# Turning the rows of the output stage by DMA, as planes of half words, in a masked attention layer on one core

## The chip, the cores and the metric

The kernel runs on one core of one Trainium2 chip. The time is device microseconds of that core. The kernel before took 671.49 us (median of 3 runs, 670.96 to 672.75). All engines and queues below are those of the one core: TensorE (PE; its weight loads are PEld), VectorE (DVE), ScalarE (ACT), GpSimd (POOL) and SyncE (SP), which only issues DMAs here.

## What is computed

One layer of a graph attention network on 2708 nodes with 1024 features, all in float32. The reference, cut to what matters:

```python
h = maximum(layernorm(x), 0)
q, k, v = h @ W_q.T + b_q, h @ W_k.T + b_k, h @ W_v.T + b_v
z = (q @ k.T) / 32 * adj
z = where(z == 0, -10000, z)
out = x + relu(softmax(z, axis=1) @ v)
```

`adj` is a 2708 x 2708 matrix of zeros and ones with about four ones in a row, so a row of the softmax has few terms that count.

## The kernel before

**What is multiplied.** The kernel never forms k and v for all nodes. It forms M = W_q^T W_k once, then for each node q' = h M, takes the products of q' with the rows of h at the node's few neighbours, and sums these rows of h with the softmax's weights: u. Then out = x + relu(u W_v^T + b_v). A list of each node's neighbours is found by searching the rows of `adj`; nodes are sorted by their number of neighbours, so that a tile of 128 nodes needs few slots. There are 21 full tiles of 128 nodes (0 to 20), and a rest of 20.

**The units.** Both products with a 1024 x 1024 matrix are made two tiles at a time, as one Strassen step of 7 products of 128 x 512 by 512 x 512 blocks (function `multiply`). One pair of tiles is a *unit*. There are ten units of queries ("q") and then ten units of outputs ("o"), and one tile on its own at the end of each kind: tile 10 for the queries, tile 11 for the outputs (`alone`, from line 1199 on). The outputs go in the pairs (8,7), (6,5), (4,3), (2,0), (1,9), (15,14), (13,12), (16,17), (20,10), (18,19), and then 11. I call the ten output units o0 to o9. Each of the 7 products is four calls of matmul on one 128 x 512 bank (`add_block`, line 898); the profile counts two instructions for each of these float32 calls, so one product is 8 rows of it.

**What turns the rows.** TensorE needs the rows transposed: features on the partitions. In the kernel before, `half_turned` (line 338) makes four TensorE transposes of 128 x 128 into one PSUM bank. `blocks` calls it four times for a unit: `upper` turns the two halves of the first tile and copies them by ScalarE to the blocks a11 and a12 (`held`, line 641); `lower` turns the second tile, copies a22 by ScalarE and leaves a21 in PSUM. Then VectorE forms s1 = a22 + a21, s3 = a11 - a21, s2 = s1 - a11, s4 = a12 - s2 (line 645). The four sums and the blocks are the stationary operands of the 7 products. For the tile alone, `turned` does both halves with two ScalarE copies (line 345). The blocks of unit n+1 are made inside unit n: `upper` at step 0, `lower` at step 2, of the steps 0 to 6 between the products (`after`).

**Where u comes from.** `attention` is a stream of VectorE steps, cut up and put between the steps of the units by `advance`, with about 19 us of it in each output unit. For each tile: the scores (line 782, one instruction of 1024 elements for a slot), the exponential by ScalarE (line 798), the weights, a first scaled row by ScalarE (line 827; for two tiles line 821), and then the sum over the other slots on VectorE (line 835). GpSimd gathers the rows of h for this by indirect DMA (line 524) and loads q' (lines 526, 759). When the sum of a tile is done, and its unit is more than two units away, GpSimd's queue stores u to `u_dram` (line 844), and SP's queue loads it again as a row tile (line 1048), in step 4 of the unit two before the one that multiplies it. If the unit is nearer (`near`), u stays in SBUF (`held`) and is turned from there: of the 21 tiles, 15 go through DRAM and 6 are held (tiles 9, 14, 12, 16, 17, 10). Row tiles have 7 buffers (`ROWS`), blocks and sums have 14 (`small`).

**Order.** The order of VectorE's instructions is written by hand throughout. From the first late unit of queries on (`n == FIRST`), the other engines and queues get their order from the scheduler of the framework, which takes instructions by program order and by when it expects their inputs. Each engine and each queue runs its own instructions in order, and waits at the first whose input isn't there.

**What ScalarE does in a unit of the output stage, beside that.** It copies the bias into the two PSUM banks of the next unit (line 670), copies partial results between banks and SBUF (lines 911, 914, 927), and applies the relu on the way out (lines 988, 992, 996, 1004). GpSimd then adds x by an accumulating gather (line 981) and scatters the rows (line 736).

Of the kernel before, what the change touches and what calls it, by code (L numbers as in the profile page):

```python
# [10 lines left out]
FT = mybir.dt.float32  # L11
U32 = mybir.dt.uint32
I32 = mybir.dt.int32
U16 = mybir.dt.uint16
AF = mybir.ActivationFunctionType
ALU = mybir.AluOpType
AX = mybir.AxisListType

P = 128
NB = 512  # L20
# [37 lines left out]
def tile_preln_masked_attention(  # L58
# [12 lines left out]
    nc = tc.nc  # L71
    N, D = x.shape
    DC = D // P
# [4 lines left out]
    FULL = N // P  # L78
# [12 lines left out]
    dram = ctx.enter_context(tc.tile_pool(name="dram", bufs=1, space=bass.MemoryType.DRAM))  # L91
# [2 lines left out]
    h_dram = dram.tile([N, D], FT, name="h_dram")  # L94
    q_dram = dram.tile([EARLY * P, D], FT, name="q_dram")
    q_late = dram.tile([(FULL - EARLY) * P, D], FT, name="q_late")
    u_dram = dram.tile([FULL * P, D], FT, name="u_dram")
    m_dram = dram.tile([2, 2, P, 4, NB], FT, name="m_dram")
    tv_dram = dram.tile([4, P, 4, NB], FT, name="tv_dram")
    bp_dram = dram.tile([1, D], FT, name="bp_dram")  # L100
# [54 lines left out]
    t = 0  # L155
    while t < NT:
# [4 lines left out]
        t = e  # L161
# [14 lines left out]
    work = ph.enter_context(tc.tile_pool(name="work", bufs=3, side="right"))  # L176
# [9 lines left out]
    def row_tile(name):  # L186
        return work.tile([P, D], FT, tag="row", name=name, bufs=ROWS)
# [145 lines left out]
    def half_turned(xt, s):  # L333

        pt = psum.tile([P, 4, P], FT, tag="tp", name="pt")
        for c in range(4):
            k = s * 4 + c
            nc.tensor.transpose(pt[:, c, :], xt[:, k * P:(k + 1) * P], ident)  # L338
        return pt

    def turned(xt, name):

        hT = work.tile([P, D], FT, tag="hT", name=f"T_{name}", bufs=2).rearrange("p (c q) -> p c q", q=P)
        for s in range(DC // 4):
            nc.scalar.copy(hT[:, s * 4:(s + 1) * 4, :], half_turned(xt, s))
        return hT

    ordered = ExitStack()
    ordered.enter_context(tc.manual_schedule(engines={mybir.EngineType.Activation, mybir.EngineType.DVE}))
# [17 lines left out]
    with tc.tile_pool(name="w", bufs=1, side="left") as wp:  # L367
# [73 lines left out]
        if True:  # L441
# [7 lines left out]
            for o in range(DC):  # L449
# [6 lines left out]
                else:  # L456
                    k = o - H
# [58 lines left out]
    half = low.enter_context(tc.tile_pool(name="half", bufs=1, side="left", reuse_waits="tile"))  # L516

    def small(name):
        return half.tile([P, NB], FT, tag="half", name=name, bufs=14)
# [8 lines left out]
    rows_of = {}  # L528
    FIRST = EARLY // 2
# [11 lines left out]
    def put(lo, hi, puts):  # L541

        for t, (t0, n) in tiles_of(lo, hi):
            put = nc.gpsimd.indirect_dma_start(  # L544
                out=tab_dram[lo >= EARLY][:, :], out_offset=bass.IndirectOffsetOnAxis(ap=pos_i[:n, t:t + 1], axis=0),
                in_=tab[:n, t, :], in_offset=None)
            for other in puts:
                tc.declare_no_dep(put.ins, other.ins, reason="rows of a permutation")
            puts.append(put)
# [81 lines left out]

    behind = []

    def blocks(xa, xb, eng=None):


        ops = {}

        def held(name, bank):
            ops[name] = small(name).rearrange("p (c q) -> p c q", q=P)  # L640
            nc.scalar.copy(ops[name], bank)  # L641

        def put(name, a, b, op, eng=None):
            ops[name] = small(name).rearrange("p (c q) -> p c q", q=P)
            step = (eng or nc.vector).tensor_tensor(ops[name], a, b, op=op)  # L645
            if eng is None:
                behind.append(step)

        def upper():
            held("a11", half_turned(xa, 0))  # L650
            held("a12", half_turned(xa, 1))

        def lower():
            held("a22", half_turned(xb, 1))
            a21 = half_turned(xb, 0)
            put("s1", ops["a22"], a21, ALU.add)
            put("s3", ops["a11"], a21, ALU.subtract)
            put("s2", ops["s1"], ops["a11"], ALU.subtract, eng)
            put("s4", ops["a12"], ops["s2"], ALU.subtract, eng)

        return ops, upper, lower
# [15 lines left out]
    ops_of = {0: blocks(*rows_of.pop(0))}  # L677
# [153 lines left out]
    def sums(t):  # L831
        u, coef = us.pop(t)
        for s in range(0 if t in EMPTY else 1, K[t]):
            fill()
            chained(lambda: nc.vector.scalar_tensor_tensor(  # L835
                u, g_of[t][s], coef[:, at[t][s]:at[t][s] + 1], u, op0=ALU.mult, op1=ALU.add))
            free.append(g_of[t][s])
            yield 1.3
        fill()
        g_of.pop(t)  # L840
        if near(t):
            held[t] = u
        else:
            nc.gpsimd.dma_start(u_dram[t * P:(t + 1) * P, :], u)
        done.add(t)

    def attention(order):
# [35 lines left out]
    def near(t):  # L883

        return any(t in unit[1:] for unit in units[:now[0] + 3] if unit[0] == "o")
# [62 lines left out]
    lo, hi = slice(0, NB), slice(NB, D)  # L948
# [87 lines left out]
    def load_rows(unit):  # L1036
        kind, *pair = unit
        rows = []
        for t in pair:
            if t in held:  # L1040
                rows.append(held.pop(t))
                continue
            rows.append(row_tile(f"{kind}r_{t}"))
            if kind == "q":
                gather(rows[-1], h_dram[:, :], t, SLOTS, P)
            else:
                assert t in done, (t, done)
                nc.sync.dma_start(rows[-1], u_dram[t * P:(t + 1) * P, :])
        return rows

    products = []
# [42 lines left out]
    for n, unit in enumerate(units):  # L1094
        kind, ta, tb = unit
        now[0] = n
        if n == FIRST:
            ordered.close()
            ordered.enter_context(tc.manual_schedule(engines={mybir.EngineType.DVE}))
            nc.sync.dma_start(bp_dram, bp_sb[0:1, :])  # L1100
        share = (20.0 if kind == "q" else 19.0) / 7
        nxt = units[n + 1] if n + 1 < len(units) else None
        results = (q_results if kind == "q" else o_results)(ta, tb)

        def after(i):
            if (n, i) == (3, 2):
                pooled.close()
                counts()
            if (n, i) == (3, 3):
                with tc.issue_after(products[-1].ins):  # L1110
                    placed.append(sort())
            if (n, i) in ((4, 1), (4, 2)):
                ts_of_wv(2 * i - 2, 2 * i)
            if n == FIRST - 1 and i == 6:

                chain.append(behind[-1])
                next(stream)
            if (n, i) >= (FIRST, 1):
                advance(share)
            if nxt is not None:  # L1120

                if n == FIRST - 1 and i in (0, 2):
                    single_turned(i // 2)
                if i == (3 if n in (0, FIRST - 1) else 0):
                    ops_of[n + 1] = blocks(*rows_of[n + 1], nc.gpsimd if n + 1 < FIRST - 1 else None)
                    if n != FIRST - 1:
                        ops_of[n + 1][1]()
                if n != FIRST - 1 and i == (4 if n == 0 else 2):
                    ops_of[n + 1][2]()
                    rows_of.pop(n + 1)  # L1130
                    if n == last_q - 1:
                        all_rows()
                if i == 3:
                    if n == FIRST - 1:
                        single["banks"] = banks_for(bp_sb)
                    else:
                        banks_of[n + 1] = banks_for(bp_sb)
                if i == 4 and n + 2 < FIRST:
                    natural_rows(n + 2)
                if i == (2 if n == FIRST else 4) and n + 2 >= FIRST and n + 2 < len(units) and n + 2 not in rows_of:  # L1140
                    while units[n + 2][0] == "o" and not done.issuperset(units[n + 2][1:]):
                        advance(1.0)
                    rows_of[n + 2] = load_rows(units[n + 2])
            if (n, i) in steps_at:
                follow(steps_at[n, i])
            if (n, i) == (3, 4):
                searched()
            if n == last_q - 1 and i == 4:

                nc.sync.dma_start(bp_sb, bv.to_broadcast([P, D]))  # L1150
                nc.vector.tensor_sub(bp_sb[:, NB:], bp_sb[:, NB:], bp_sb[:, :NB])

            for k, at in enumerate(((0, 0), (0, 1), (0, 3), (0, 4), (0, 5), (0, 6), (1, 2))):
                if (n - last_q, i) == at:
                    place, src = ((M[:, 0, 0], of_wv(0, 0)), (T[:, 0], tv_dram[0]), (T[:, 1], tv_dram[1]),
                                  (M[:, 1, 0], of_wv(1, 0)), (M[:, 1, 1], of_wv(1, 1)), (T[:, 2], tv_dram[2]),
                                  (T[:, 3], tv_dram[3]))[k]
                    nc.sync.dma_start(place, src)

        multiply(n, results, after)  # L1160
# [39 lines left out]
    send(gather(y, x, alone, SLOTS, P))  # L1200
    tail(NT - 1)
    r, = load_rows(("o", alone))
    uT = turned(r, "alone")
    X, Z = banks_for(bp_sb)
    add_block(X, uT[:, 0:4, :], M[:, 0, 0])
    p1 = small("p1")
# [191 lines left out]
```

## Time and profile before

The profiled execution took 671.25 us in all, with a span of 669.5 us from the first to the last instruction; the 1.75 us around it are outside the trace. The granted TensorE clock was 0.997.

| What | Number |
|---|---|
| median of 3 runs (lowest, highest) | 671.49 us (670.96, 672.75) |
| the profiled execution, its span | 671.25 us, 669.5 us |
| VectorE busy | 518.4 us (77%) |
| ScalarE busy | 266.2 us (40%) |
| GpSimd busy | 403.1 us (60%) |
| moved by DMA | 194.29 MB, 290 GB/s |
| 120 + 48 transposes of rows u | lines "pt<-ident,or" and "pt<-ident,u" |

How to read it: a group of instructions is named by its line in the kernel, its engine, its operation, and what it writes and reads ("ps<-M,a" writes the bank ps, reads the matrix M and the block a). "xN" is the number of instructions. Matmuls overlap each other, so the mean of one (593 ns for 512 columns, 273 ns for a transpose) is longer than the distance between two of them (429 ns and 109 ns, from the chain: 8 of them in 3.43 and 0.87 us). The chain of work that ended last is followed from the last instruction back: at each step to what released it, or to the instruction before it on its engine.

### The profile page before, as it was taken

To read this page: it belongs to the slowest core of one execution; us is meant where nothing else is said; L and a number is where in the kernel's file an instruction comes from. 1 tells how busy PE (TensorE), PEld (TensorE's weight loads), DVE (VectorE), ACT (ScalarE), POOL (GpSimd) and SP (SyncE) were. 2 spreads that over 40 slices of the span, in tenths; PEclk is the share of its full clock that TensorE was granted. 3 is DMA by queue.
4 is the path that set the end of the run, shared out by engine and by line. 5 is a ranking of instruction groups with operands and counts; after the bars stand their busy time and mean duration, and the time that the engine had idled before them with its cause. 6 is when DMAs were issued, how large, how long until landed. Compare 5 with 4: busy or idle time off the path is not lost.

```text
span 669.5 us, 6372 instructions
## 1 busy us (share of the span) xinstructions
PE 653.4 (98%) x1764; PEld 332.4 (50%) x1764; DVE 518.4 (77%) x998; ACT 266.2 (40%) x399; POOL 403.1 (60%) x397
## 2 busy tenths in 40 slices
PE   7999999999999999999999999999999999999994
PEld 4777776444444444444444444444444444444441
DVE  5999879999589402799988899798788989989201
ACT  3467985855844212232242231432332433322220
POOL 2559991585513778676666366574674877872342
PEclk9999999999999999999999999999999999999998
DMA  8997989699566877799999999998997899794653
GB/s 344 407 360 262 368 302 374 235 372 352 204 218 227 279 242 229 270 373 348 326 340 352 403 411 386 293 306 247 333 294 191 235 304 356 212 284 141 175 136 117
DMA packets 62452, 194.29 MB, mean 290 GB/s; under 512 B 9721, under 2 KB 10073, under 8 KB 61514
## 3 DMA queue, kind: packets, MB, share of 16 engines
q0 software_dynamic: 34608, 109.77, 50.0%
q1 hardware_dynamic: 26794, 80.89, 32.5%
q10 hardware_dynamic: 1008, 3.15, 1.2%
q8 instruction: 16, 0.26, 0.2%
q14 instruction: 26, 0.21, 0.1%
HBM read 161.38 MB, written 45.46 MB: 309 GB/s over the span
## 4 chain that ended last, share of the span: by engine, by line
PE 83%; DVE 6%; issue 4%; DMA 3%; POOL 2%; ACT 1%; POOLq 0%; DVEq 0%
PE ps L898 37%; PE psy L898 26%; PE ps_y L397 6%; PE ps_x L397 5%; PE pt L338 4%; PE ps_z L397 4%; DVE junk L782 2%; DVE u L835 2%; DMA g<-h_dram,tab 2%; POOL g L524 1%; DMA out_dram<-y,tab 1%; DVE s L645 1%; DMA wlow<-in_wk_dram 1%; ACT a L641 0%; ACT u L827 0%
## 5 line engine op out<-in xcount | busy, mean ns | idle before, releaser
L524 POOL DMA_INDIRECT g<-h_dram,tab x106 | 129.9, 1226 | 46.7 <-issue 23.4
L898 PE MATMUL psy<-wlow,s 128*128 128x512 f32 x320 | 144.2, 593 | 1.3 <-ACT u L927 1.3
L898 PE MATMUL ps<-M,a 128*128 128x512 f32 x320 | 144.1, 593 | 0.1
L782 DVE SCALAR_TENSOR_TENSOR junk<-g,pq 128x1024 uint8<-128x1024 f32 x94 | 115.1, 1225 | 14.7 <-DMA pq<-q_dram,tab 12.6
L835 DVE SCALAR_TENSOR_TENSOR u<-g,coef,u 128x1024 f32<-128x1024 f32 x78 | 100.0, 1282 | 7.9 <-ACT u L827 4.9
L898 PEld LDWEIGHTS psy<-wlow,s 128*128 128x128 f32 x320 | 59.2, 190 | 69.4 <-issue 66.8
L898 PEld LDWEIGHTS ps<-M,a 128*128 128x128 f32 x320 | 59.3, 190 | 68.0 <-issue 67.2
L320 DVE FIND_INDEX8 at<-ones,adj 128x8 uint32<-128x685 f32 (+1 forms) x88 | 74.4, 865 | 0.0
L898 PE MATMUL psy<-wlow,a 128*128 128x512 f32 x160 | 72.3, 595 | 1.2 <-DVE q L963 0.8
L898 PE MATMUL ps<-wlow,s 128*128 128x512 f32 x160 | 72.1, 593 | 0.8 <-DVE s L645 0.7
L898 PE MATMUL ps<-M,s 128*128 128x512 f32 x160 | 71.9, 592 | 0.0
L981 POOL DMA_INDIRECT y<-in_x_dram,tab x21 | 37.0, 1763 | 49.2 <-ACT y L996 23.1
L309 ACT ACTIVATE sized<-adj 128x2708 uint8<-128x2708 f32 (+1 forms) x22 | 54.2, 2465 | 4.2 <-DMA adj<-in_adj_dram 4.1
L898 PEld LDWEIGHTS psy<-wlow,a 128*128 128x128 f32 x160 | 30.0, 190 | 40.3 <-issue 34.2
L898 PEld LDWEIGHTS ps<-wlow,s 128*128 128x128 f32 x160 | 30.2, 190 | 39.8 <-issue 37.1
L898 PEld LDWEIGHTS ps<-M,s 128*128 128x128 f32 x160 | 30.3, 190 | 37.6 <-issue 37.1
L257 POOL TENSOR_TENSOR hsum<-hsum,x 128x1024 f32<-128x1024 f32 (+1 forms) x17 | 40.3, 2371 | 0.4
L645 DVE TENSOR_TENSOR s<-a,pt 128x512 f32<-128x512 f32 x40 | 25.6, 682 | 17.5 <-ACT a L641 9.2
L641 ACT COPY a<-pt 128x512 f32<-128x512 f32 x60 | 33.2, 593 | 4.9 <-issue 3.3
L544 POOL DMA_INDIRECT tab_dram<-tab,pos_i x22 | 22.6, 1028 | 20.2 <-DVE pos_i L608 13.8
L827 ACT ACTIVATE u<-g,coef 128x1024 f32<-128x1024 f32 x16 | 18.4, 1148 | 34.8 <-DVE coef L826 26.8
L736 POOL DMA_INDIRECT out_dram<-y,tab x21 | 25.1, 1195 | 8.9 <-issue 5.8
(230 smaller groups left out, 871.6 us busy)
## 6 DMA issues: line engine op xcount, KB each, us to landing
adj<-in_adj_dram SPq DMA_DIRECT2D x21, 1354.0 KB
x<-in_x_dram SPq DMA_DIRECT2D x21, 512.0 KB
h_dram<-x POOLq DMA_DIRECT2D x21, 512.0 KB
u_dram<-u POOLq DMA_DIRECT2D x15, 512.0 KB
or<-u_dram SPq DMA_DIRECT2D x15, 512.0 KB
q_late<-q SPq DMA_DIRECT2D x10, 512.0 KB
pq<-q_late POOLq DMA_DIRECT2D x10, 512.0 KB
g<-in_wv_dram SPq DMA_DIRECT2D x16, 256.0 KB
```

The lines of the kernel that those rows point to most:

```text
L257: nc.gpsimd.tensor_add(hsum[:n], hsum[:n], xt[:n])
L309: nc.scalar.activation(sized[:n], a[:n, :, :PW], AF.Abs, accum_out=total[:n, t:t + 1])
L320: nc.vector.max_index(at[:n, t - first_t, g, :], ones[:n, 0:8], a[:n, g, :])
L338: nc.tensor.transpose(pt[:, c, :], xt[:, k * P:(k + 1) * P], ident)
L397: mm = nc.tensor.matmul(bank, a_tile(o + H * a[0], a[1], i), b(o), start=first and o == 0, stop=(o == H - 1), skip_group_check=True)
L524: return nc.gpsimd.indirect_dma_start(out=dst, out_offset=None, in_=src, in_offset=off, bounds_check=N - 1, oob_is_err=False)
L641: nc.scalar.copy(ops[name], bank)
L645: step = (eng or nc.vector).tensor_tensor(ops[name], a, b, op=op)
L782: chained(lambda: nc.vector.scalar_tensor_tensor(junk, g_of[t][s], 1.0, tq[t], op0=ALU.mult, op1=ALU.mult, accum_out=zall[:, t, s:s + 1]))
L835: chained(lambda: nc.vector.scalar_tensor_tensor(u, g_of[t][s], coef[:, at[t][s]:at[t][s] + 1], u, op0=ALU.mult, op1=ALU.add))
L898: mm = nc.tensor.matmul(bank, a[:, c, :], b[:, c, :], start=False, stop=(c == 3), skip_group_check=True)
L981: return nc.gpsimd.indirect_dma_start(out=y[:n], out_offset=None, in_=x, in_offset=off, compute_op=ALU.add)
```

## The change

The rows u are no longer turned by TensorE. When the sum u of a tile is done, ScalarE makes two copies of 128 x 1024 half words: the float32 words are looked at as pairs of 16-bit words, and all upper half words go to the left half of a second row tile (`split`), all lower half words to its right half. `split` is held or stored where u was; `u_dram` becomes a tensor of 16-bit words with rows of 2048. `load_rows` now issues a transposing DMA on SP's queue for every tile of an output unit, from DRAM or, for a held tile, from `split` in SBUF, into a new row tile: 16 blocks of 128 x 128 half words, the first 8 with the upper half words of the turned tile, the other 8 with the lower. `words_joined` puts the two planes together again: two ScalarE copies for each block of 128 x 512 words, each writing every second half word. `blocks_turned` takes the place of `blocks` for output units: eight such copies make a11, a12, a22 and a21, where three ScalarE copies from PSUM made a11, a12 and a22; a21 gets a buffer of `small` of its own. VectorE's four sums stay, with a21 read from SBUF and not from PSUM. For the tile alone, two copies of 128 x 1024 half words take the place of two copies from PSUM. The units of queries are turned by TensorE as before.

```diff
-    u_dram = dram.tile([FULL * P, D], FT, name="u_dram")
+    u_dram = dram.tile([FULL * P, 2 * D], U16, name="u_dram")
...
+    def words_joined(dst, turned, lo, hi):
+
+        words = dst.bitcast(U16).rearrange("p (k w) -> p k w", w=2)
+        for w in (1, 0):
+            nc.scalar.copy(words[:, :, w], turned[:, (1 - w) * D + lo:(1 - w) * D + hi])
+
+    def blocks_turned(ta, tb):
...
+        def joined_half(name, turned, s):
+            half = small(name)
+            words_joined(half, turned, s * NB, (s + 1) * NB)
+            ops[name] = half.rearrange("p (c q) -> p c q", q=P)
...
+        def upper():
+            joined_half("a11", ta, 0)
+            joined_half("a12", ta, 1)
+
+        def lower():
+            joined_half("a22", tb, 1)
+            joined_half("a21", tb, 0)
+            put("s1", "a22", "a21", ALU.add)
+            put("s3", "a11", "a21", ALU.subtract)
+            put("s2", "s1", "a11", ALU.subtract)
+            put("s4", "a12", "s2", ALU.subtract)
...
+        split = row_tile(f"split_{t}").bitcast(U16)
+        words = u.bitcast(U16).rearrange("p (k w) -> p k w", w=2)
+        for w in (1, 0):
+            nc.scalar.copy(split[:, (1 - w) * D:(2 - w) * D], words[:, :, w])
         if near(t):
-            held[t] = u
+            held[t] = split
         else:
-            nc.gpsimd.dma_start(u_dram[t * P:(t + 1) * P, :], u)
+            nc.gpsimd.dma_start(u_dram[t * P:(t + 1) * P, :], split)
...
         for t in pair:
-            if t in held:
-                rows.append(held.pop(t))
-                continue
             rows.append(row_tile(f"{kind}r_{t}"))
...
-                nc.sync.dma_start(rows[-1], u_dram[t * P:(t + 1) * P, :])
+                rows[-1] = rows[-1].bitcast(U16)
+                nc.sync.dma_start_transpose(rows[-1].rearrange("p (c r) -> p c r", r=P),
+                                            held.pop(t) if t in held else u_dram[t * P:(t + 1) * P, :])
...
-                    ops_of[n + 1] = blocks(*rows_of[n + 1], nc.gpsimd if n + 1 < FIRST - 1 else None)
+                    ops_of[n + 1] = blocks_turned(*rows_of[n + 1]) if nxt[0] == "o" else \
+                        blocks(*rows_of[n + 1], nc.gpsimd if n + 1 < FIRST - 1 else None)
...
-    uT = turned(r, "alone")
+    uT = work.tile([P, D], FT, tag="hT", name="T_alone", bufs=2)
+    words_joined(uT, r, 0, D)
+    uT = uT.rearrange("p (c q) -> p c q", q=P)
```

More of the change, by code (lines that the diff above doesn't have):

```diff
@@ L339, in half_turned @@
         return pt
[L341 to L346, printed above, removed]
     ordered = ExitStack()
@@ L632, in tile_preln_masked_attention, with put @@
     behind = []
+    def words_joined(dst, turned, lo, hi):
[3 more added lines that the diff above has]
+    def blocks_turned(ta, tb):
+        ops = {}
+        def joined_half(name, turned, s):
+            half = small(name)
+            words_joined(half, turned, s * NB, (s + 1) * NB)
+            ops[name] = half.rearrange("p (c q) -> p c q", q=P)
+        def put(name, a, b, op):
+            ops[name] = small(name).rearrange("p (c q) -> p c q", q=P)
+            nc.vector.tensor_tensor(ops[name], ops[a], ops[b], op=op)
+        def upper():
[8 more added lines that the diff above has]
+            put("s4", "a12", "s2", ALU.subtract)
+        return ops, upper, lower
     def blocks(xa, xb, eng=None):
```

## The prediction

> **What bounds the kernel now.** I read the page's shares first, then the chain that ended last, VectorE's waits, ScalarE's groups, and last the DMA queues. The page:
>
> ```profile
> PE 653.4 (98%) x1764; PEld 332.4 (50%) x1764; DVE 518.4 (77%) x998; ACT 266.2 (40%) x399; POOL 403.1 (60%) x397
> ...
> PE 83%; DVE 6%; issue 4%; DMA 3%; POOL 2%; ACT 1%; POOLq 0%; DVEq 0%
> ```
>
> TensorE is busy for 98% and makes 83% of the chain. The chain from 511 us on, in order of time (start, length, what):
>
> ```profile
> 511.36 0.69 DVE u L995
> ...
> 572.87 0.61 DVE p L991
> 573.53 3.70 PE psy L898 x8
> 577.23 0.88 PE pt L338 x8
> 578.10 3.43 PE psy L898 x8
> 581.54 0.88 PE pt L338 x8
> 582.41 6.87 PE ps L898 x16
> ...
> 642.65 0.93 PE pt L338 x8
> ```
>
> Two things are to be seen. From 573 on it is products and transposes without a gap: 8 transposes are 0.88 us of the path, twice in a unit. From 511 to 573 the chain runs through VectorE, and yet TensorE was idle for only 0.34 us at its end (573.53): in these 2.4 units both engines need the same time. VectorE's waits from 366 us (where the first rows u are turned) to 521, then from 521 to 625 (us in total, times, longest):
>
> ```profile
> DVE u L995 <- PE ps L898: 5.9, 4, 1.6
> DVE s L645 <- ACT a L641: 4.0, 3, 2.1
> DVE u L835 <- ACT u L827: 3.7, 3, 1.3
> DVE s L645 <- PE pt L338: 1.9, 1, 1.9
> DVE q L966 <- PE ps L898: 1.6, 1, 1.6
> DVE p L991 <- PE psy L898: 0.7, 3, 0.2
> ```
>
> ```profile
> DVE u L835 <- ACT u L827: 3.6, 3, 1.2
> DVE u L835 <- ACT u L821: 1.2, 1, 1.2
> ```
>
> Before 521 VectorE waits 5.9 + 1.9 + 1.6 + 0.7 = 10.1 us for TensorE, and 4.0 us for copies of turned blocks, which themselves follow TensorE. After 521 it waits for TensorE no more. So VectorE has 14.1 us in hand, and TensorE has most to give. No line has VectorE waiting for a gather.
>
> **What goes.** Each output unit has 16 transposes, 2 x 0.875 = 1.75 us of TensorE; ten units, 17.5 us, and 0.93 us for the tile alone: **18.4 us**, were TensorE the only bound. What is late next is VectorE. From the timeline, the step that frees TensorE for the last product of o8 (line 991) ended at 619.8, and TensorE started that product at 625.37. TensorE's new start, ahead by the nine units' and the query unit's transposes, is 625.37 - 17.5 = 607.9. VectorE without the 14.1 us of waits would be there at 605.7. But it can't use all of them: laying its work by units beside the new 24.03 us of a unit (56 x 0.429), it is still early by 1.1, 1.8 and 0.8 us in o2 to o4, so 3.7 us stay as waits, and it gets there at 609.4. The gain at that point is 625.37 - 609.4 = 16.0 us, and with the 0.9 us of the tile alone **16.9 us**.
>
> **What is added to ScalarE.** ScalarE's groups from 366 to 625 us give the prices:
>
> ```profile
> L641 ACT COPY a<-pt 128x512 f32<-128x512 f32 x30 | 16.6, 592 | 0.0
> L670 ACT COPY ps<-bp_sb 128x512 f32<-128x512 f32 x20 | 12.0, 602 | 0.3
> L827 ACT ACTIVATE u<-g,coef 128x1024 f32<-128x1024 f32 x10 | 11.5, 1147 | 9.0 <-DVE coef L826 5.5 <-DVE m L825 2.5 <-DMA g<-h_dram,tab 1.1
> ```
>
> The first group is what goes, 30 copies. No row copies half words, or with a step of two. Nearest are 0.60 us for 512 elements (line 670) and 1.05 for 1024 (line 221, 1050 ns, SBUF to SBUF). I take these, one element at a time whatever its size. Half of it would follow if bytes counted, twice if a step of two cost two; neither shows in a row. In this window ScalarE was busy 84 of 259 us. Added: 14 of the 21 tiles' splits (the first seven sums end before 366), 28 x 1.05 = 29.4; 80 halves joined, 80 x 0.59 = 47.2; gone, 30 x 0.59 = 17.7. That makes 143 us of some 243, 59% where it was 32%. ScalarE alone would bind only if each half-word copy cost 2.3 times the row.
>
> Its bulk lies beside other work; its order does not. A split waits for the last sum of VectorE with all behind it in ScalarE's queue, and two splits are 2.1 us. Behind them stand the evictions that TensorE needs (lines 911, 914, 927, with 6.9 to 10 us until the bank is used again, two or three products of 3.43) and the first scaled row (line 827), for which VectorE stands idle. In 366 to 625 VectorE waits for that row 7 times, 8.5 us in all, each time just its length. With ScalarE busy for 59%, I add one split's length to each: 7 x 1.0 = **7 us**; none is the lower end, both splits before each of the 14 first rows of the window, 14 x 2.1 = 29 us, the upper. The joins are hidden: rows u arrive a unit ahead (loaded from 344 us, turned at 370; from 386, turned at 422), they no longer wait for TensorE, and the 4.0 us of waits for line 641 are in the sum above already. If they are joined just before VectorE's s1 all the same, 2.4 us for a22 and a21 in place of one copy costs 1.8 us in each unit, 18 us.
>
> **What moves in the queues.** GpSimd's store waits for two splits more (2.1 us), and behind it in that queue stand gathers; they run some instructions ahead of VectorE, which waited for none, so zero, with a gather's issue (1.2 us) in each of 21 tiles, 25 us, as the upper end. Row tiles: 6 are asked for in a unit, where 4 were, out of 7; a tile lives for about 0.7 of a unit, so they go round. Six more loads of 512 KB go through SP's queue, which waits idle for the stores anyway.
>
> **The transposing load** is the unknown. A plain load of 512 KB, in a quiet stretch (the DMA queues from 628 to 636):
>
> ```profile
> q1 hardware_dynamic: 144, 0.52, 17.6%
> ```
>
> It was issued at 628.36 and moved from 629.2 to 631.0: 1.8 us. That is the lower end. For the upper end the nearest row of small pieces is the reload of the sorted table (line 554): 10 tiles x 128 = 1280 pieces of 72 bytes, issue done at 232.0, arrived at 237.8, so 5.8 us or 4.5 ns a piece among other traffic. The destination has 16 blocks of 128 half words for each row, 2048 pieces of 256 bytes: 9.3 us; 18.6 if each is paid on both sides. I take 4 us, near the plain load, since the number of bytes is the same. The tightest rows are those of tile 12: by counting line 835 its sum ends at 522.8, and VectorE's s1 comes after 535. Split 2.1, load 0.9 + 4, two joins 2.4: 9.4 us, within 12. It adds nothing up to 6.6 us a load, and 3 us at 9.3. Other held tiles have 14 us or more.
>
> The Trainium skill, *DMA: Bandwidth & Descriptors*, section "Latency and other measured facts", gives a transposing DMA 261 GB/s with a non-contiguous middle dimension; by that, as an estimate, 512 KB take 2.0 us and the sum is 661.5 us; by the small pieces of line 554, 9.3 us, it is 664.5. The trace of before has no such transfer, so it can't decide between them.
>
> **The sum.** 671.25 - 16.9 + 7 = 661.4 us against the profiled execution; that stands 0.24 us under the median shown, so I say **661.5 us**.
>
> **Rivals.**
> 1. *TensorE is the only bound* (part of the forecast's case): ScalarE's copies fall into its idle time. 671.25 - 18.4 = 652.9 us, the floor. For it: 68% idle. Against: VectorE and TensorE tie from 511 to 573.
> 2. *ScalarE's order eats it all.* With 1 us at each of the 7 waits, and half of the 18 us at s1: -16.9 + 16 = -1, 670 us, no change.
> 3. *ScalarE becomes the bound's supplier* (slower): VectorE waits at all 14 first rows and all ten s1, 24 places. It decides from 16.9 / 24 = 0.7 us a place. At a split's 1.05 us in each, +25 - 16.9 = +8, 680 us; with the pair, 705. For it: queue order is fixed, splits wait for VectorE, and VectorE has no slack after 511. Against: ScalarE is idle before most of its copies now (line 996: 35 us).
> 4. *The transposing load is the bound* (slower). It decides at 24.03 / 2 = 12 us a tile. At 18.6 us, ten pairs from 344 us on end at 344 + 372 = 716; from the last pair's transposes (607) to the end there are now 62 us: 778 us. For it: the stretch's DMA engines are 92 to 94% busy. Against: they carried 289 to 319 GB/s there, and over 400 in other slices. The Trainium skill speaks for this rival: *VectorE: DVE Perf Modes*, section "The three transpose paths", gives 1309 ns for a 128 x 128 block by DMA and 390 by TensorE, and 16 such blocks in a row would be an estimated 21 us a tile, 825 us in all; here TensorE's 109 ns between transposes already stand against its second figure.
>
> That the transposes stay on TensorE is no rival: the output units no longer call them.
>
> **How the numbers follow.** Forecast with its floor, 652 to 669 us: 0.52. No change: 0.10. ScalarE's order, slower: 0.20. The load as the bound: 0.18. Less than 0.3%, 2 us, can't be told from no change. So faster 0.52, same 0.10, slower 0.38. The forecast's own range is 652 to 669; 8 in 10 takes in the first three cases and reaches to 705, where rival 3 ends at a pair of splits.
>
> **What would show it.** Right: no "pt" rows after 370 us but those of queries; products 3.43 us apart with no gap from 370 to 510; line 827's waits of VectorE at 2 us each, seven or so; the new copies at 0.6 and 1.05 us; line 645 waiting for ScalarE no longer than now. Wrong: SP's queue or ScalarE's joins waiting for the transposing load (rival 4); VectorE idle before lines 835 and 645 for over 17 us more than now (rival 3); half-word copies of twice the row; gathers that VectorE waits for.

## The result and the profile after

The changed kernel takes **780.4 us** (median of 4 executions, 771.07 to 787.62), the kernel before, measured beside it, 672.0 us (670.96 to 672.75). Two of the four count as slow (787.62 and 783.95 us), and the ratio of 1.152 [1.144, 1.160] is that of the other two, 776.86 and 771.07 us, whose mean of **774.0 us** is what the experiments below are compared with. The forecast was 661.5 us with a range to 705, so both miss. The profiled execution is the longest, 787.62 us (span 785.9). Terms that are read from its trace stand against 671.25 us, a difference of 116.4 us, of which 13.6 are that execution's distance from 774.0.

The page of the changed kernel: engines, the clock that TensorE was granted, the DMA engines' busy tenths and GB/s in 40 slices, the packets, the hardware queue, and the chain by engine.

```profile
PE 657.9 (84%) x1596; PEld 321.3 (41%) x1596; DVE 518.4 (66%) x998; ACT 340.6 (43%) x491; POOL 401.8 (51%) x397
...
PEclk9999999999999999999899599959978986979898
DMA  9979996966686879999999979999989999989374
GB/s 350 407 279 360 302 368 257 356 251 233 213 296 215 312 266 341 350 269 239 234 419 359 259 200 221 140 228 158 244 202 266 140 193 199 127 208 187 94 168 134
DMA packets 103970, 197.40 MB, mean 251 GB/s; under 512 B 53161, under 2 KB 53513, under 8 KB 103034
...
q1 hardware_dynamic: 68314, 84.04, 41.9%
...
PE 35%; DMA 31%; issue 14%; DVE 10%; ACT 4%; POOL 3%; SPq 2%; POOLq 0%; DVEq 0%; ACTq 0%
```

TensorE is no longer the bound: 35% of the chain where it had 83%, and DMA has 31% where it had 3%. The last 18 slices are the ones to look at. The DMA engines stay at seven to nine tenths until the last three, but what they move falls from some 300 GB/s to 94 to 266. Their being busy does not say that they move much. There are 43440 small packets more than before, 432 besides the 21 x 2048 pieces of 256 bytes that the prediction counted.

The chain that ended last, from 470 us on (start, length, what):

```profile
477.24 27.08 DMA y<-in_x_dram,tab
506.46 20.61 DMA g<-h_dram,tab
...
540.65 20.98 DMA y<-in_x_dram,tab
...
603.09 45.30 DMA or<-split x2
...
656.39 33.92 DMA or<-split
...
698.51 29.76 DMA or<-u_dram
```

Two single transposing loads hold the chain for 34 and 30 us, and the gathers that feed VectorE and the skip rows of the output last over 20 us; in the kernel before, VectorE waited for no gather from 285 us on. VectorE's, TensorE's and ScalarE's waits from 285 us on (us in total, times, longest):

```profile
DVE s L645 <- ACT a L631: 43.6, 6, 15.3
DVE junk L809 <- DMA g<-h_dram,tab: 28.9, 3, 17.4
DVE u L862 <- ACT u L854: 26.6, 7, 14.7
```

```profile
PE psy L929 <- ACT u L958: 30.2, 2, 22.3
PE ps L929 <- ACT ps L697: 28.9, 3, 12.1
PE psy L929 <- DMA wlow<-tv_dram: 18.0, 1, 18.0
PE ps L929 <- DVE s L645: 13.0, 1, 13.0
```

```profile
ACT split L871 <- DVE u L862: 59.9, 17, 20.2
ACT a L631 <- DMA or<-split: 55.3, 4, 16.0
ACT w L825 <- DVE junk L809: 43.9, 9, 20.1
ACT a L631 <- DMA or<-u_dram: 34.9, 4, 17.7
```

(Lines have moved: 929 is the old 898, the products; 854 and 862 the old 827 and 835; 809 the old 782; 825 the old 798, the exponential; 645 is s1 to s4; 631 the joins, 871 the splits, 1077 the loads.) Read from the bottom: ScalarE's joins wait 90 us for transposing loads, and most of the copies that TensorE needs (lines 958 and 697) stand behind them in ScalarE's queue. The longest wait, 22.3 us for line 958, does not: there ScalarE stood 20.1 us at the exponential, which waited for VectorE's scores, and these for a gather (17.4 us). So the loads reach TensorE in two ways, through the joins and through late gathers. TensorE is idle in waits for 112.1 us in all (those four lines, 90.1, and five smaller ones, 22.0); before, it was 0.3 us. SP's queue is held too; the loads' own issue instructions (ns, min/median/max):

```profile
L1077 SPq DMA_TRANSPOSE or<-u_dram x15: 2073/6867/23852, 344.4 to 748.3; - x15
L1077 SPq DMA_TRANSPOSE or<-split x6: 3538/15606/24949, 487.3 to 656.4; - x6
```

In the kernel before, a plain load's issue took 0.32 us (0.55 at most). Behind the transposing loads stand SP's other loads; TensorE's 18.0 us for `wlow<-tv_dram` and 13 us of VectorE's for the bias `bp_sb` are theirs. And TensorE is slower after its waits: by the timeline, the next eight products took 5.1 to 6.3 us after each wait of 5 us or more, 3.7 after waits of 2.5 us, and 3.6 with none. The mean granted clock is 0.931 where it was 0.997. The new copies, and the group of products that lost most:

```profile
L929 PE MATMUL psy<-wlow,a 128*128 128x512 f32 x160 | 80.7, 651 | 34.7 <-DMA wlow<-tv_dram 18.0
...
L631 ACT COPY a<-or 128x512 uint16<-128x512 uint16 x80 | 53.8, 757 | 90.1 <-DMA or<-split 55.3
...
L871 ACT COPY split<-u 128x1024 uint16<-128x1024 uint16 x42 | 42.1, 1041 | 63.2 <-DVE u L862 59.9
```

That group took 72.3 us before; the four groups that grew (148.0, 146.1, 80.7 and 78.4 where they were 144.2, 144.1, 72.3 and 72.1) make +20.5 us. So on TensorE: +111.8 of waits, +20.5 of slower products, -18.4 of transposes = +113.9 of the 116.4 us.

### The profile page after: what moved, and what is told of

It is laid out like the page before. It is cut to its first block, busy times and chain, and to the rows that moved or that the text cites. A ratio compares the mean times of both kernels' runs of the same rounds, so it can differ in the third digit from the quotient of the medians.

```text
span 785.9 us, 6164 instructions
## 1 busy us (share of the span) xinstructions
PE 657.9 (84%) x1596; PEld 321.3 (41%) x1596; DVE 518.4 (66%) x998; ACT 340.6 (43%) x491; POOL 401.8 (51%) x397
## 4 chain that ended last, share of the span: by engine, by line
PE 35%; DMA 31%; issue 14%; DVE 10%; ACT 4%; POOL 3%; SPq 2%; POOLq 0%; DVEq 0%; ACTq 0%
PE ps L929 11%; DMA or<-split 10%; PE psy L929 9%; DMA y<-in_x_dram,tab 6%; PE ps_y L390 5%; DMA or<-u_dram 5%; DMA g<-h_dram,tab 5%; PE ps_x L390 4%; PE ps_z L390 3%; DVE at L320 2%; DVE u L862 2%; SPq L1077 2%; DVE junk L809 2%; PE pt L338 2%; POOL g L517 2%
## 5 line engine op out<-in xcount | busy, mean ns | idle before, releaser
L929 PE MATMUL psy<-wlow,s 128*128 128x512 f32 x320 | 148.0, 604 | 35.5 <-ACT u L958 31.3
L929 PE MATMUL ps<-M,a 128*128 128x512 f32 x320 | 146.1, 599 | 12.2 <-ACT ps L697 12.1
L809 DVE SCALAR_TENSOR_TENSOR junk<-g,pq 128x1024 uint8<-128x1024 f32 x94 | 115.2, 1225 | 43.3 <-DMA g<-h_dram,tab 28.9
L929 PE MATMUL psy<-wlow,a 128*128 128x512 f32 x160 | 80.7, 651 | 34.7 <-DMA wlow<-tv_dram 18.0
L929 PE MATMUL ps<-wlow,s 128*128 128x512 f32 x160 | 78.4, 636 | 30.5 <-ACT ps L697 16.8
L631 ACT COPY a<-or 128x512 uint16<-128x512 uint16 x80 | 53.8, 757 | 90.1 <-DMA or<-split 55.3
L871 ACT COPY split<-u 128x1024 uint16<-128x1024 uint16 x42 | 42.1, 1041 | 63.2 <-DVE u L862 59.9
L929 PEld LDWEIGHTS psy<-wlow,a 128*128 128x128 f32 x160 | 32.8, 210 | 80.7 <-issue 57.0
L929 PEld LDWEIGHTS ps<-wlow,s 128*128 128x128 f32 x160 | 32.3, 205 | 74.1 <-issue 53.3
L645 DVE TENSOR_TENSOR s<-a,a 128x512 f32<-128x512 f32 x20 | 12.9, 688 | 43.6 <-ACT a L631 43.6
L537 POOL DMA_INDIRECT tab_dram<-tab,pos_i x22 | 22.6, 1028 | 20.1 <-DVE pos_i L601 13.7
```

The lines of the kernel that those rows point to most:

```text
L631: nc.scalar.copy(words[:, :, w], turned[:, (1 - w) * D + lo:(1 - w) * D + hi])
L809: chained(lambda: nc.vector.scalar_tensor_tensor(junk, g_of[t][s], 1.0, tq[t], op0=ALU.mult, op1=ALU.mult, accum_out=zall[:, t, s:s + 1]))
L871: nc.scalar.copy(split[:, (1 - w) * D:(2 - w) * D], words[:, :, w])
L929: mm = nc.tensor.matmul(bank, a[:, c, :], b[:, c, :], start=False, stop=(c == 3), skip_group_check=True)
```

## Experiments

Two theories stand after the result. **A**: the transposing load, through the DMA engines, is the whole loss. **B**: ScalarE's copies and their order in its queue (the prediction's third rival) make it or a good part of it. The waits can't tell them apart, because "ScalarE waits for a load, TensorE for ScalarE" looks alike in both.

### e1_plain: the same kernel with plain loads

```diff
-nc.sync.dma_start_transpose(rows[-1].rearrange("p (c r) -> p c r", r=P), held.pop(t) if ...)
+nc.sync.dma_start(rows[-1], held.pop(t) if ...)
```

> The changed kernel with plain loads of the two planes in place of the 21 transposing loads: same bytes, same queue, same ScalarE copies and waits. It leaves out the turning, so the outputs are not the layer's. Theory A (the transposing load is slow and slows the gathers beside it): 655 to 670 us, the forecast's sum without its failed term. Theory B (ScalarE's splits and joins stand ahead of what TensorE and VectorE need): it stays above 730 us.

Measured 666.93 us (10 runs) beside 672.84, ratio 0.993 [0.991, 0.995]. All copies of ScalarE are there, in the same order, and all of the loss is gone, so B falls. VectorE's waits in this run:

```profile
DVE u L862 <- ACT u L854: 12.7, 7, 2.8
...
DVE s L645 <- ACT a L631: 5.7, 4, 3.1
```

Seven waits for the first scaled row, 1.8 us each on average, are what the prediction forecast. The run is also the forecast's sum without its unknown term: 666.7 in the profiled execution where 661.4 was worked out. TensorE's last product ends at 653.1 instead of 660.8, 7.6 us earlier (9.9 forecast: 7.4 us of TensorE's waits stay, from the 5.7 us above among others), and behind it the tail is 3.1 us longer: the last output rows waited for TensorE's last product before, and now they wait for GpSimd, which still has other rows to write.

### e2_nojoin: no joining copies

```diff
-half = small(name)
-words_joined(half, turned, s * NB, (s + 1) * NB)
-ops[name] = half.rearrange("p (c q) -> p c q", q=P)
+ops[name] = turned.bitcast(FT)[:, s * NB:(s + 1) * NB].rearrange("p (c q) -> p c q", q=P)
```

> The changed kernel without the 82 joining copies: the products read the turned half words as they are, and both planes are filled with the upper half words so that no value is infinite. It leaves out the joining, so the outputs are not the layer's. Theory A: 740 to 785 us, since TensorE and VectorE wait for the transposing loads themselves. Theory B: 690 to 720 us, since 90 us of ScalarE's waits stand at these copies.

Measured 780.1 us (one execution): nothing is won by taking out 82 copies. The wait moves; with nothing to join, the splits and VectorE wait for the loads themselves:

```profile
ACT split L869 <- DMA or<-split: 81.1, 4, 36.5
```

So the joins are where the lateness shows, not where it comes from.

### e3_half: half the bytes turned

```diff
-nc.scalar.copy(words[:, :, w], turned[:, (1 - w) * D + lo:(1 - w) * D + hi])
+nc.scalar.copy(words[:, :, w], turned[:, lo:hi])
...
-nc.sync.dma_start_transpose(rows[-1].rearrange(...), ... u_dram[t * P:(t + 1) * P, :])
+nc.sync.dma_start_transpose(rows[-1][:, :D].rearrange(...), ... u_dram[t * P:(t + 1) * P, :D])
```

> The changed kernel with the upper plane alone turned (8 blocks of 128 x 128 half words in place of 16); the joins copy it twice, so ScalarE's work is the same. It leaves out the lower half words. Theory A: half of the small packets, so about half of the loss comes back, 700 to 730 us. Theory B: 765 to 785 us, nothing of ScalarE's order has changed.

Measured 719.2 us (one execution). That is 52 us above e1_plain's 666.9, where the change stands 107 us above it (774.0). Half of each load costs half: the loss goes with the bytes turned, not with the number of loads or waits.

### e4_dram: all rows by way of DRAM

```diff
-if near(t):
-    held[t] = split
-else:
+if True:
     nc.gpsimd.dma_start(u_dram[t * P:(t + 1) * P, :], split)
```

> The changed kernel with every tile stored to DRAM and turned from there, none from SBUF. Theory C (the six loads that read SBUF are the slow ones, 16 us at the median of issue against 7): 700 to 740 us. Theory A: 765 to 800 us, the load is slow from either place and six stores are added.

Measured 760.4 us (one execution), between the two cases, 14 us under 774.0, while the change's own executions differ by 17 us. That a source in SBUF is worse than one in DRAM isn't shown.

### e5_quiet and e7_price: the load by itself

Both put chains of loads behind the last output, e7_price some gathers also.

```diff
+for k in range(4):
+    nc.sync.dma_start_transpose(r.rearrange("p (c r) -> p c r", r=P), u_dram[:P, :])
+for k in range(4):
+    nc.sync.dma_start_transpose(twin.rearrange("p (c r) -> p c r", r=P), r)
```

> The changed kernel with twelve loads added behind the last output, one after the other into the same row tiles: four transposing ones from DRAM, four transposing ones from SBUF, four plain ones from DRAM. Nothing else runs by then. Theory A, price part: a quiet transposing load takes 6 to 8 us from issue to landing from either place, and a plain one 2.5 to 3 us. Theory C: from SBUF it takes 15 us or more. Should the price be 15 us from both, there is no contention to explain, only the price.

> The changed kernel with DMAs added behind the last output, in a chain: four plain loads of a tile, four transposing loads from DRAM, four transposing copies from SBUF, each alone; then ten gathers of 128 rows alone; then nine gathers beside three transposing loads from DRAM; then nine beside three transposing copies from SBUF. Contention (theory A in its second form): alone, a transposing load moves its 512 KB in 2.5 to 4 us and the gathers move at 350 GB/s or more; together they take far longer than the sum, three transposing loads and nine gathers over 40 us where 9 x 1.4 + 3 x 3.5 = 23 us would do. Plain sharing: 20 to 25 us.

They took 830.9 and 915.8 us (one execution each), which says nothing by itself; the chains are what is read. In e5_quiet the four loads from SBUF (line 1253):

```profile
L1253 SPq DMA_TRANSPOSE twin<-or x4: 1517/1838/1956, 795.1 to 807.9; - x4
...
DMA to landing us min/median/max: 4.3/4.3/4.3
```

The chain from DRAM still ran beside the last outputs there. In e7_price it was alone: 4.4 us from issue to landing, up to 290 GB/s in a slice, and 4.3 us from SBUF at 205 to 220 GB/s. The prediction took 0.9 + 4 us. **The load's length alone was sized right.** In the same run the gathers had been put in another order than meant, so its other half shows nothing; e11_price does that again.

### e6_beside: the load without a reader

The kernel before, with a transposing load into a spare tile that nobody reads behind each of its 15 plain loads of rows u. TensorE still turns them; nothing waits for the new loads but the tiles' next users and what stands behind them in SP's queue.

```diff
 nc.sync.dma_start(rows[-1], u_dram[t * P:(t + 1) * P, :])
+spare = row_tile(f"spare_{t}").bitcast(U16)
+nc.sync.dma_start_transpose(spare.rearrange("p (c r) -> p c r", r=P),
+                            u_dram.bitcast(U16)[t * P:(t + 1) * P, :])
```

> The kernel before, with TensorE's transposes, and behind each of its 15 plain loads of rows u a transposing load of the same rows into a spare row tile that nobody reads. Theory A: these loads share the DMA engines with the gathers, so gathers take twice as long and VectorE waits for them: 690 to 740 us. If only the load's own length matters (its readers wait, nobody else does): 671 to 680 us.

Measured 744.5 us (4 runs), ratio 1.107 [1.105, 1.109]: 72 us for 15 loads, 4.8 us each, somewhat above A's span and far from a cost of its own length only. What VectorE waits for:

```profile
DVE u L835 <- ACT u L827: 32.2, 7, 24.9
DVE junk L782 <- DMA g<-h_dram,tab: 19.8, 4, 8.9
DVE junk L782 <- DMA M<-h_dram,tab: 19.3, 2, 15.2
```

Gathers are late for which VectorE did not wait in this part before, though no instruction waits for a transposed byte. The spare loads took 7.4/21.7/35.4 us to land (min/median/max), at the median five times their length alone. TensorE's longest waits have another way in:

```profile
PE psy L898 <- DMA wlow<-tv_dram: 25.3, 2, 21.7
```

These are the loads of W_v's products, which stand behind the spare loads in SP's queue. So the 4.8 us hold both, the time taken from gathers and the time that SP's queue is held. No run issues the transposing loads from another queue, so the two aren't told apart in the kernel; e11_price, whose gathers come from GpSimd's queue, shows the first by itself.

### e10_skip, e8_late, e9_alone: fewer tiles by DMA

In these, TensorE turns some tiles u as before and the DMA the rest: the last 15 tiles in e10_skip, three late ones in e8_late, only the tile alone in e9_alone.

```diff
+def by_dma(t):
+    return order.index(t) >= 6      # e8_late: t in (18, 19, 11); e9_alone: t == 11
```

> The changed kernel with the first three output units (tiles 8, 7, 6, 5, 4, 3) turned by TensorE as before, and the other 15 tiles by DMA. In the changed kernel TensorE waits 18 us for a load of products of W_v that stands behind transposing loads in SP's queue, and 8 us at the query unit beside it, both before 460 us; these go. If the loss is one price per transposing load, 15 of 21 leave about 75 of 108 us: 745 us. If the early loads weigh more, since SP's other loads stand behind them: 715 to 735 us.

> The changed kernel with only the last output unit (tiles 18, 19) and the tile alone (11) turned by DMA, all others by TensorE as before. TensorE saves 1.75 + 0.93 = 2.7 us. If a transposing load costs little where few gathers run, 668 to 670 us against 671.5. If two loads beside the last gathers still slow them, VectorE is late at the last sum: 672 to 685 us.

> The changed kernel with only the tile alone (11) turned by DMA, all others by TensorE as before. Its load runs when no gathers of neighbours are left. TensorE saves 0.93 us and the turned rows arrive before TensorE is free: 670 to 671 us, which can't be told from no change. Contention would show nothing here, and any loss would be the load's own length on the path: 672 to 676 us.

e10_skip took 739.6 us (one execution): 67 us for 15 tiles, 4.5 us each, beside the 4.8 of e6_beside and the 4.9 (102 / 21) of the change. So it is much nearer to one price per load than to early loads weighing more. e8_late took 674.8 us beside 671.4, ratio 1.0052 [1.0037, 1.0067], and e9_alone 670.35 us (12 runs), 0.9987 [0.9969, 1.0004], which can't be told from no change. In e8_late's chain a gather of the output's skip rows is late once again, and the last load itself, that of tile 11, holds the chain:

```profile
552.62 8.04 DMA y<-in_x_dram,tab
...
630.35 9.39 DMA or<-u_dram
```

How the 3.4 us divide between the two isn't shown.

In e9_alone the one load is issued behind the last gathers that VectorE needs (601.5 us), and it costs nothing that can be measured; but only 0.9 us of transposes can be saved there.

### e11_price: the same gathers beside each kind of load

Behind the last output, in order: ten gathers of 512 KB alone, then the same ten beside four plain loads, beside four transposing loads from DRAM, and beside four from SBUF. Each load writes the tile of the one before, so they follow one another.

```diff
+for load in (None, lambda: nc.sync.dma_start(yw, rs), lambda: nc.sync.dma_start_transpose(yt, rs),
+             lambda: nc.sync.dma_start_transpose(yt, r)):
+    if load is not None:
...
+        for k in range(4):
+            load()
+        mark = gather(slots[8], h_dram[:, :], 0, 0, P)
+    for k in range(8):
+        with tc.issue_after(mark.ins):
+            mark = gather(slots[k], h_dram[:, :], 0, k % 4, P)
```

> The changed kernel with DMAs added behind the last output, this time with the gathers held in order: two plain loads, two transposing loads from DRAM, two transposing copies from SBUF, each alone; nine gathers of 512 KB alone; then the same gathers beside four plain loads; beside four transposing loads from DRAM; beside four transposing copies from SBUF. From the run before: 4.4 us from issue to landing for a quiet transposing load from DRAM, 4.3 from SBUF. Contention: the nine gathers alone and beside plain loads run near their issue, 1.3 us apart, some 13 to 20 us in all; beside transposing loads over 30 us, with the rate of all DMA together falling under 200 GB/s, below that of either kind alone. Plain sharing: 20 us beside transposing loads too, at over 290 GB/s.

The four stretches (window, length, busy time of PE, PEld, DVE, ACT and POOL, then clock, DMA share and GB/s):

```profile
808.00:825.00 17.00, 0.00 (x0) 0.00 (x0) 0.00 (x0) 0.00 (x0) 9.13 (x10) 0.50 0.83 308
829.00:848.00 19.00, 0.00 (x0) 0.00 (x0) 0.00 (x0) 0.00 (x0) 9.35 (x10) 0.50 0.96 357
854.00:890.00 36.00, 0.00 (x0) 0.00 (x0) 0.00 (x0) 0.00 (x0) 9.39 (x10) 0.50 0.94 198
895.00:932.00 37.00, 0.00 (x0) 0.00 (x0) 0.00 (x0) 0.00 (x0) 9.40 (x10) 0.50 0.86 199
```

The run took 937.2 us (one execution); again only the stretches are read. From the first issue to the next stretch's first copy they are 17.6, 22.4, 37.9 and some 37 us. A plain load adds (22.4 - 17.6) / 4 = 1.2 us to the stretch; a transposing one adds 20.3 / 4 = 5.1 us from DRAM and 4.9 from SBUF. That is a little more than its whole length alone: the two kinds hardly share the DMA engines, although the engines show as 94% busy.

A stretch ends with its last load, though, and not with its last gather. The chain of the loads from DRAM (start, length):

```profile
853.55 6.43 DMA y_alone<-u_dram
860.00 21.40 DMA y_alone<-u_dram
881.41 5.51 DMA y_alone<-u_dram
886.94 4.43 DMA y_alone<-u_dram
```

By the DMA queues' packets the gathers ended near 885, so the fourth load ran alone, in 4.4 us. The gathers themselves took 17 us alone, 20 beside plain loads and 31 beside these, so the three loads that ran among them cost them some 14 us, between 4 and 5 us each. The prediction treated the length as latency that other work covers; it is time taken from the gathers.

### e12_small: the same small pieces, not turned

What is left is whether the small pieces do it. Here each transposing load becomes two plain ones, of the even and of the odd blocks.

```diff
-nc.sync.dma_start_transpose(rows[-1].rearrange("p (c r) -> p c r", r=P), src)
+dst = rows[-1].rearrange("p (c h r) -> p h c r", h=2, r=P)
+src = src.rearrange("p (c h r) -> p h c r", h=2, r=P)
+for h in range(2):
+    nc.sync.dma_start(dst[:, h], src[:, h])
```

> The change with each transposing load replaced by two plain loads, one of the even and one of the odd blocks of 128 half words, so that the same 2048 pieces of 256 bytes move and nothing is turned (the turning is left out, the output units multiply rows in place of columns). Theory A, the number of small pieces is what slows the DMA engines beside the gathers: the small packets of the page stay near 53000 and the time near that of the change, 740 to 785 us. Theory B, it is the turning itself, whatever the pieces: near the run with one plain load, 665 to 685 us, though the small packets are the same. In between, 690 to 730, both have a part.

Measured 684.3 us (4 runs) beside 672.4, ratio 1.018 [1.011, 1.024]. The packets of this run:

```profile
DMA packets 103971, 197.41 MB, mean 288 GB/s; under 512 B 53161, under 2 KB 53513, under 8 KB 103034
...
q1 hardware_dynamic: 68314, 84.04, 36.5%
```

They are those of the change, to one packet. Of the 107 us between one plain load (666.9) and the change (774.0), the pieces with their second issue make 17.4 us, and the turning itself 89.7 us, 4.3 us for each of 21 loads.

## Why the prediction was wrong

**What failed** is the step "It adds nothing up to 6.6 us a load". It set the load's length against the slack of the tile that waits for it. The length was right (4.4 us taken alone, 4 + 0.9 forecast), and e11_price shows what the step left out: beside gathers the load takes about 5 us of what the DMA engines can do, however long its reader can wait. The prediction had the number that makes this dear: the stretch's DMA engines were 92 to 94% busy. It set that aside in rival 4, since "they carried 289 to 319 GB/s there, and over 400 in other slices". For plain loads that argument is good (1.2 us each in e11_price). For transposing ones it is not: 21 x 5 us are 105 us, and 6 to 8% of the 281 us from 344 to 625 are, as an estimate, 17 to 22 us.

The step on the queues said VectorE "waited for none" of the gathers, and from it that their queue costs nothing. It waited for none before; with the loads it waits 28.9 us, and in e6_beside, where only the loads are added, 39 us.

**Rival 4** named the mechanism, the load as the bound, and its time of 778 us stands beside 780.4 (and 774.0). But it came to that figure by 18.6 us a tile in a row, from small pieces paid twice. The measured parts are others: 4.3 to 4.4 us alone, up to 34 us among gathers (single loads of the chain), some 5 us each off the whole. The agreement in the sum is partly luck. With a chance of 0.18 it was left out of the range, whose end at 705 came from rival 3.

The prediction's estimate of 21 us a tile took 16 times the 1309 ns that the Trainium skill, *VectorE: DVE Perf Modes*, section "The three transpose paths", gives for one 128 x 128 block by DMA. It leant to the right side, but alone 16 blocks in one load took 4.4 us. The Trainium skill, *Advanced Engine Details and Errata*, section "X-Bar Transpose (TRN2)", states that "TRN2 transpose DMAs are as fast as regular DMAs". In the quiet chain of e11_price that is nearly so: 4.5 us from one transposing load from DRAM to the next, 4.1 for plain ones (3.4 in e5_quiet). Beside gathers it is not: 5.1 us against 1.2.

**What goes** was right in kind. The transposes left the path, and e1_plain shows 7.6 us at TensorE's last product where 16.9 - 7 = 9.9 was forecast. **ScalarE's order** was sized right: seven waits of 12.7 us in all in e1_plain, with 8.5 + 7 = 15.5 forecast. Rival 3, on which most of the chance of "slower" lay, did not happen.

**The copies**: the splits, 1.041 us, were taken at 1.05. The joins, taken at 0.59, took 0.757. Reading every second half word costs nothing extra; writing every second one costs 28%. At 80 joins that is 13 us of ScalarE, and in e1_plain VectorE waits 5.7 us for them at s1, where the prediction called them hidden.

**What moves in the queues** was counted as six loads more on SP. Their number did not matter; the time of their issue did. At 0.32 us an issue the queue was free; at 2 to 25 us an issue W_v's products and the bias came late (18 and 13 us).

**The signs** did their work: "SP's queue or ScalarE's joins waiting for the transposing load" and "gathers that VectorE waits for" are both in the waits above, and "half-word copies of twice the row" is not. One sign pointed at the wrong place: VectorE's waits for lines 854 and 645, given to rival 3, grew by 18 and 39 us, but through loads and gathers that came late: in e1_plain they are back to 12.7 and 5.7.

**Open.** Why a transposing load keeps gathers from the engines isn't shown; the traces give packets and their times, and the packets of e12_small are alike. How much of the loss in the kernel comes through late gathers and how much through SP's queue isn't shown either. Whether SBUF as a source is worse (14 us, e4_dram) is within the spread of the change. Loads held back until no gather runs were tried only for the tile alone. No version here is faster than the kernel before by more than e1_plain's 0.7%, and that one leaves the turning out.

## What to carry to other kernels

Ask of a transfer not only how long it takes and who waits for it, but what it takes from transfers beside it; where the DMA engines are 90% busy, a hidden load is hidden only if it shares. A transfer of a kind that the trace has never shown beside the kernel's own traffic can be tried without a reader, as in e6_beside: three lines of code separated its price from the copies and the order that the change also brings. And when two engines' waits point at each other, replace the suspected transfer by a plain one first, before looking into the queues.

## What the hardware showed

- Ten gathers (5.2 MB) with four loads (2.1 MB) move at 357 GB/s when the loads are plain and at 198 when they turn (e11_price, the windows shown; 207 while the gathers last), though gathers alone run at 308 and transposing loads alone reach 205 to 290 in a slice. The busy share of the DMA engines doesn't tell: 0.96 and 0.94.
- The issue instruction of a transposing load holds SP's queue for 1.5 to 2.4 us in quiet and for 2.1 to 24.9 us in the changed kernel; a plain load's took 0.32 us at the median in the kernel before.
- Pieces of 256 bytes that are not turned cost little, 17.4 us for 43000 of them with 21 issues more (e12_small), 0.4 ns each, where the prediction's upper end was 4.5 ns a piece.
- ScalarE's copy of half words takes 1.04 us for 1024 when it reads with a step of two, and 0.757 us for 512 when it writes with a step of two.
